# The first expert's rows: read back from slots, or gathered from the normalised tokens

## The chip, the core and the metric

The kernel runs on one core of a Trainium2 chip. The metric is device time in microseconds (us) of one execution, a median over runs. Five engines matter, each with an instruction queue of its own: PE (matrix products and transposes into PSUM banks), DVE (VectorE), ACT (ScalarE), POOL (GpSimd, which issues the indirect DMAs) and SP (SyncE, which issues the ordinary DMAs).

## What is computed

Two layers over 800 tokens (8 batches of 100) of width 512. Layer 0 is a cross attention and then a mixture of experts; layer 1 is a second cross attention and a quantised feed-forward. The change touches the mixture alone:

```python
scores = einsum('btd,ed->bte', layernorm(x), Wg)        # 8 experts
topk_s, topk_i = top_k(scores, 2); probs = softmax(topk_s)
for e in range(8):
    h = silu(xn @ W1[e].T) * (xn @ W2[e].T)             # 352 hidden
    y = y + w[..., e:e+1] * (h @ W3[e].T)
x = x + y
```

## The kernel before

The tokens stand in 7 tiles of 128 rows (the last has 32). The gate handles them in two groups, tiles 0 to 4 and tiles 5 and 6, so that the first group's work lies beside the last projections of attention 0.

For each group `gate_norm` (L583) writes the rows to `x_acc` in DRAM on SP (L585) and normalises them into `x_all` on DVE (L586). `gate_columns` and `gate_scores` make the scores on PE, `rank_choices` the two best experts of every token on DVE. `give_slots` (L677) then counts with two kinds of 0/1 products on PE (L682, L686) how many tokens chose each expert before this one, turns that into a slot number (`nb`, `slot`, `to`, L695 to L719 on DVE), and `scatter` (L699) has POOL write each tile's rows, once per choice, to their slots of the DRAM tensor `x_slot`: 10 indirect DMAs for the first group, 3 for the second (L700). Every expert owns 240 slots of 516 numbers: the 512 normalised values, two gate numbers, the rank and the token's number.

Between these steps stands the "fold", independent work for the second attention: for pairs of heads, `fold_first` (L732), `fold_turn` (L744), `fold_second` (L750) and `fold_third` (L761) alternate a few products on PE with a copy out of PSUM on ACT (L741, L748, L758, L765). The fold fills PE's time while the gate's small DVE chain runs. The order of PE, DVE and ACT is written out by hand in this region (`manual_schedule`); SP and POOL get theirs from the framework's planner, which places an instruction by its place in the program and the time it expects it to be ready.

After the second group's slots, one product counts all tokens per expert (L844); `most` and `spilt` (L846, L848) say if an expert got more than 240. All engines load `spilt` (L929) and branch on it (L936); the branch is not taken on these inputs. Behind the branch SP reads the slots of experts 0 and 1 back from `x_slot` (`fetch`, L1035, L1038), then loads the first weights to quantise (L874, L879). PE finishes the last fold (L1113 to L1116) and turns expert 0's rows to columns (`columns_of`, L1058, transposes at L1063, copies at L1065 and L1067). `choices` (L1043) makes the gate factor and the token number of each slot on DVE.

The loop over experts (L1119) does 48 products of 240 columns (L1126) and 12 of 512 (L1187) each, fetches expert e+2's slots, turns expert e+1's rows (L1165), quantises some weights of the last feed-forward on DVE, and adds the results into `x_acc` by indirect DMAs on POOL (L1199). Four row tiles (`slot_rows`, L920) hold the slots of two experts; the fetch for e+2 waits until the readers of expert e's tiles are done.

Of the kernel before, what the change touches and what calls it, by code (L numbers as in the profile page):

```python
# [50 lines left out]
def tile_kernel(  # L51
# [486 lines left out]
    def gate_col(tag, dtype=F32):  # L538
        return gp.tile([P, NT], dtype, tag=tag, name=tag)
# [39 lines left out]
    ms = [gate_col(f"m{k}") for k in range(2)]  # L579
    tops = [x_all[:, :, D + 2], gate_col("top1")]  # L580
    probs = [gate_col("p0"), x_all[:, :, D + 1]]

    def gate_norm(t):  # L583
        r = ROWS[t]
        nc.sync.dma_start(x_acc[ds(t * P, r), :], xs[t][:r])  # L585
        nc.vector.tensor_scalar(  # L586
            x_all[:r, t, :D], xs[t][:r], mvs[:r, t, 0:1], rstd_all[:r, t : t + 1],
            ALU.subtract, ALU.mult,
        )

    gate_in = []

    def gate_columns(t0, t1):
        if t0 == 0:
# [42 lines left out]
    def rank_choices(t0, t1):  # L639
# [34 lines left out]
        nc.vector.tensor_tensor(p2[:, g], p2[:, g], p1[:, g], ALU.mult)  # L674
        nc.vector.tensor_tensor(x_all[:, g, D], p1[:, g], p2[:, g], ALU.subtract)

    def give_slots(t0, t1):  # L677
# [18 lines left out]
        nc.vector.scalar_tensor_tensor(  # L696
            nb[:, g, :], counts, float(CAP), nb[:, g, :], ALU.is_lt, ALU.mult
        )
        def scatter(t, k, r):  # L699
            d = nc.gpsimd.indirect_dma_start(  # L700
                out=x_slot,
                out_offset=bass.IndirectOffsetOnAxis(ap=to_i[k][:r, t : t + 1], axis=0),
                in_=x_all[:r, t, :], in_offset=None,
            )
# [5 lines left out]
        n = t1 - t0  # L710
        nc.vector.tensor_tensor(
            tmp[:, :, g, :], hot[:, :, g, :],
            nb[:, g, :].unsqueeze(1).to_broadcast([P, 2, n, NE]), ALU.mult,
        )
        nc.vector.tensor_reduce(slot[:, :, g], tmp[:, :, g, :], AX.X, ALU.add)
        nc.vector.scalar_tensor_tensor(
            unfit[:, :, g], slot[:, :, g], 0.0, spill[:, :, g], ALU.is_equal, ALU.mult
        )
        nc.vector.tensor_tensor(to[:, :, g], unfit[:, :, g], slot[:, :, g], ALU.add)  # L719
        for k in range(2):  # L720
            for t in range(t0, min(t1, NT - 1)):
                scatter(t, k, ROWS[t])

        if t1 == NT:
            r = ROWS[-1]
            nc.vector.tensor_copy(x_all[ds(r, r), NT - 1, :], x_all[:r, NT - 1, :])
            nc.vector.tensor_copy(to_i[0][ds(r, r), NT - 1 :], to_i[1][:r, NT - 1 :])
            scatter(NT - 1, 0, 2 * r)

    def fold_first(t_p, *pairs):  # L732
        pa = bank()
        for n, (i, wq_p, kq_p, qr_p) in enumerate(pairs):
            for c in range(CQ // P):
                for j in range(2):
                    nc.tensor.matmul(
                        pa[ds(R1 * j, R1), ts(n, P)], qr_p[:, j, c, :], kq_p[:, j, c, :],
                        start=(c == 0), stop=(c == CQ // P - 1),
                    )  # L740
        nc.scalar.copy(t_p, pa[:, : 2 * P])  # L741
        return [(i, wq_p) for i, wq_p, _, _ in pairs], t_p
# [8 lines left out]
    def fold_second(i, wq_p, a_p):  # L751
        pb = bank()
        for j in range(2):
            nc.tensor.matmul(
                pb[ds(R1 * j, R1), :], a_p[:, ts(j, R1)], wq_p[:, j, :], start=True, stop=True
            )
# [66 lines left out]
    nc.scalar.activation(sd0[:, 0:1], ln_eps, AF.Exp)  # L823
    for t in range(5, 7):
        gate_norm(t)
    u3 = fold_first(turned[2], loaded.pop(0), loaded.pop(0))
    u2 = fold_turn(*u2)
    f0 = fold_second(*u1[0])
    xT = gate_columns(5, 7)
    u3 = fold_turn(*u3)  # L830
    f1 = fold_second(*u1[1])
    for i in (6, 7):
        loaded.append(fold_load(i))
    gate_scores(5, 7, xT, lambda: fold_third(*f0))
# [7 lines left out]
    pn = bank()  # L842
    for n, some in enumerate((first_group, both[:, 5, :], both[:, 6, :])):
        nc.tensor.matmul(pn[:, :NE], ones_bf, some, start=(n == 0), stop=(n == 2))  # L844
    most = small.tile([P, 1], F32, tag="most", name="most")
    nc.vector.tensor_reduce(most, pn[:, :NE], AX.X, ALU.max)  # L846
    spilt = gp.tile([P, 1], I32, tag="spilt", name="spilt")
    nc.vector.tensor_scalar(spilt, most, float(CAP), None, ALU.is_gt)  # L848
    f2 = fold_second(*u3[0])
    fold_third(*f1)  # L850
    turned = fw.tile([P, 2 * P], F32, tag="a_p", name="turned3", bufs=1)
    u4 = fold_first(turned, loaded.pop(0), loaded.pop(0))
# [56 lines left out]
    HC = len(SLOTS)  # L909
    GB = 3  # L910

    def quantise_next():
# [121 lines left out]

    def fetch(e, tiles=None):  # L1035
        got = []
        for i, xg in enumerate(tiles or slot_tiles(e)):
            d = nc.sync.dma_start(xg, x_slot[ds(1 + e * CAP + SLOTS[i][0], SLOTS[i][1]), :])  # L1038
            got.append((xg, d.ins))
        return got  # L1040

# [16 lines left out]
    def columns_of(e, got):  # L1058
        xgT = ffw.tile([P, KC, CAP], F32, tag="xgT", name=f"xgT{e}")
        for i, (s0, n) in enumerate(SLOTS):  # L1060
            pt = bank().rearrange("p (c q) -> p c q", c=KC)
            for c in range(KC):
                nc.tensor.transpose(pt[:, c, :n], got[i][0][:, ts(c, P)], ident[:n, :n])  # L1063
            if i % 2:
                nc.vector.tensor_copy(xgT[:, :, ds(s0, n)], pt[:, :, :n])  # L1065
            else:
                nc.scalar.copy(xgT[:, :, ds(s0, n)], pt[:, :, :n])  # L1067
        return xgT
# [7 lines left out]
    def load_wo(*heads):  # L1076
        for i in heads:
# [785 lines left out]
```

## Time and profile before

| what | us |
|---|---|
| median of 3 runs (lowest, highest) | 655.17 (654.39, 655.68) |
| the profiled execution's own time | 656.77 |
| its span, first to last instruction | 653.6 |
| PE busy in the span | 626.9 (96%) |
| DVE, ACT, POOL busy | 415.6, 242.4, 177.3 |
| span from 112 to 147.3 (the gate's end, up to expert 0's first product) | 35.3 |
| PE busy in 122 to 130 | 2.26 of 8.00 |
| PE busy in 135 to 141 | 4.28 of 6.00 |

Times are us from the span's first instruction. In a line of the timeline the first column is the start, the second how long the piece took, then come engine, line of the kernel, operation, what is written and read, and the number of instructions; in brackets stands the idle time of the engine before it and what ended it. PE's ends are modelled from the size of the product; the start of the engine that waited for the product is measured.

### The profile page before, as it was taken

How to read it: one execution, taken by the hardware profiler on the slowest of the kernel's cores; microseconds unless marked ns; L12 is line 12 of the kernel's file. 1: busy time of each engine (PE TensorE's matmuls, PEld its weight loads, DVE VectorE, ACT ScalarE, POOL GpSimd, SP SyncE). 2: the span in 40 equal slices, each digit the busy share in tenths (PEclk: the TensorE clock that was granted, in tenths of full speed). 3: DMA queues.
4: the chain of work that ended last, by engine and by line, in shares of the span. 5: the costliest groups of instructions: out<-in, count | busy, mean ns of one | idle time of the engine just before them, and what ended most of it. 6: DMA issues, size and time to landing. Idle time of an engine off the chain costs nothing.

```text
span 653.6 us, 9865 instructions
## 1 busy us (share of the span) xinstructions
PE 626.9 (96%) x3468; PEld 404.3 (62%) x3475; DVE 415.6 (64%) x1046; ACT 242.4 (37%) x554; POOL 177.3 (27%) x190
## 2 busy tenths in 40 slices
PE   9999999589999999999999999999999999999995
PEld 6767756347777776578866766666666544444442
DVE  4865688227777553245068877877676457666787
ACT  3653455351111111332255655555555213222130
POOL 1232430610222211128623234233243002222020
PEclk9999999799999999999999999999999999999998
DMA  8990184937999999553300212010000301011211
GB/s 294 306 253 18 57 265 142 308 118 237 295 297 328 286 258 299 120 184 113 89 1 17 61 44 61 17 37 12 1 12 0 127 11 26 20 20 30 51 38 65
DMA packets 80290, 80.34 MB, mean 123 GB/s; under 512 B 41267, under 2 KB 54119, under 8 KB 80111
## 3 DMA queue, kind: packets, MB, share of 16 engines
q1 hardware_dynamic: 76543, 70.97, 36.9%
q0 software_dynamic: 3696, 8.72, 5.9%
q8 instruction: 28, 0.46, 0.3%
q14 instruction: 23, 0.19, 0.1%
HBM read 56.36 MB, written 16.50 MB: 111 GB/s over the span
## 4 chain that ended last, share of the span: by engine, by line
PE 66%; DVE 6%; POOL 1%; DMA 1%; ACT 1%; issue 1%; ACTq 0%; SPq 0%; POOLq 0%; DVEq 0%
PE bank L384 12%; PE bank L1432 10%; PE bank L1126 9%; PE bank L1407 8%; PE bank L1349 7%; PE bank L1187 5%; PE bank L1424 5%; PE bank L1593 3%; PE bank L1227 2%; PE bank L1388 2%; DMA dn<-in_wdn 1%; POOL e L1418 1%; PE bank L1063 1%; DVE nm L1411 1%; DVE amax L152 1%
## 5 line engine op out<-in xcount | busy, mean ns | idle before, releaser
L1418 POOL TENSOR_SCALAR e<-e,rs 128x361 f32<-128x361 f32 x51 | 61.2, 1201 | 121.2 <-DVE rs L1417 85.0
L384 PE MATMUL bank<-wvo,ctxT 128*128 128x512 f32 x192 | 84.2, 593 | 0.0
L1407 PE MATMUL bank<-kvT,qe 128*128 128x361 f32 (+1 forms) x208 | 78.9, 475 | 0.9 <-ACT qe L1394 0.9
L1126 PE MATMUL bank<-xgT,w 128*128 128x240 f32 (+1 forms) x384 | 74.1, 369 | 0.4 <-ACT xgT L1067 0.4
L1126 PEld LDWEIGHTS bank<-xgT,w 128*128 128x128 f32 (+1 forms) x384 | 64.7, 181 | 11.5 <-issue 6.2
L1432 PE MATMUL bank<-pT,kvr 121*128 121x400 f32 x192 | 70.6, 503 | 0.0
L1415 ACT ACTIVATE e<-bank,nm 128x361 f32<-128x361 f32 x100 | 56.4, 564 | 33.4 <-DVE nm L1411 24.1
L1411 DVE TENSOR_REDUCE nm<-bank 128x1 f32<-128x361 f32 x100 | 52.7, 528 | 17.4 <-PE bank L1407 16.6
L1424 PEld LDWEIGHTS bank<-ident,e 128*121 128x121 f32 x300 | 46.6, 184 | 26.9 <-POOL e L1418 3.9
L384 PEld LDWEIGHTS bank<-wvo,ctxT 128*128 128x128 f32 x192 | 36.0, 190 | 42.1 <-issue 41.7
L1199 POOL DMA_INDIRECT x_acc<-y,place x16 | 24.7, 1542 | 108.1 <-ACT y L1198 105.4
L1610 POOL TENSOR_TENSOR hid<-g,u 128x512 f32<-128x512 f32 (+1 forms) x17 | 20.5, 1214 | 112.6 <-ACT g L1601 74.8
L1424 PE MATMUL bank<-ident,e 128*121 128x128 f32 x300 | 49.6, 275 | 1.0 <-POOL e L1418 1.0
L1432 PEld LDWEIGHTS bank<-pT,kvr 121*128 121x128 f32 x192 | 33.9, 190 | 20.6 <-ACT pT L82 0.9
L349 POOL TENSOR_TENSOR s<-s,rs 100x800 f32<-100x800 f32 x16 | 24.4, 1522 | 69.6 <-DVE rs L348 35.3
L1187 PE MATMUL bank<-w,hT 128*128 128x512 f32 (+3 forms) x96 | 42.9, 594 | 0.3 <-DVE hT L1150 0.3
L1407 PEld LDWEIGHTS bank<-kvT,qe 128*128 128x128 f32 (+1 forms) x208 | 32.1, 186 | 11.3 <-ACT qe L1394 2.2
L82 ACT COPY pT<-bank 121x384 f32<-121x384 f32 (+3 forms) x55 | 24.3, 442 | 25.0 <-PE bank L1424 24.4
L80 DVE COPY ctxT<-bank 128x400 f32<-128x400 f32 (+2 forms) x23 | 13.2, 572 | 30.5 <-PE bank L1349 24.9
L80 DVE COPY pT<-bank 121x384 f32<-121x384 f32 (+3 forms) x57 | 28.7, 503 | 2.3 <-PE bank L1424 2.3
L1349 PE MATMUL bank<-xT,wqf 128*128 128x256 f32 (+1 forms) x128 | 29.8, 393 | 0.0
L1593 PE MATMUL bank<-w1q,xqT 128*128 128x512 bf16 (+1 forms) x140 | 29.2, 361 | 0.4 <-DMA xqT<-xq 0.2
(267 smaller groups left out, 1002.8 us busy)
## 6 DMA issues: line engine op xcount, KB each, us to landing
w<-in_w SPq DMA_DIRECT2D x8, 1408.0 KB
gu<-in_wgu SPq DMA_DIRECT2D x22, 256.0 KB
wq_p<-in_wq SPq DMA_DIRECT2D x8, 512.0 KB
w<-in_w SPq DMA_DIRECT2D x16, 256.0 KB
wo<-in_wo SPq DMA_DIRECT2D x8, 512.0 KB
x_slot<-zeros SPq DMA_DIRECT2D x1, 3840.0 KB
kq_p<-in_wkcq SPq DMA_DIRECT2D x16, 192.0 KB
dn<-in_wdn SPq DMA_DIRECT2D x4, 704.0 KB
```

Of the source, the lines that this page charges most:

```text
L80: nc.vector.tensor_copy(dst, src)
L384: nc.tensor.matmul(po[:, :D], lhs[:, c, ds(t * P, r)], rhs[:, c, :], start=(c == 0), stop=(c == chunks - 1),)
L1126: nc.tensor.matmul(po, w12_e[:, c, cols], xgT[:, c, :], start=(c == c0), stop=(c == c1 - 1))
L1187: nc.tensor.matmul(py[i][:n], hT[:mr, m, ds(s0, n)], w3_e[:mr, m, :], start=(m == blocks[0]), stop=(m == blocks[2]),)
L1349: nc.tensor.matmul(pq[:, i, :], wqf[:, c, ts(p0 + i, P)], xT[:, c, :], start=(c == 0), stop=(c == KC - 1),)
L1407: nc.tensor.matmul(ps[ds(to, n), :L], qe[:, ds(k0, n)], kvT, start=True, stop=True)
L1411: d = nc.vector.tensor_reduce(nm[:r], ps[:r, :L], AX.X, ALU.max, negate=True)
L1415: nc.scalar.activation(e[:r], ps[:r, :L], AF.Exp, bias=nm[:r], accum_out=sm[:r])
L1418: (nc.vector if odd else nc.gpsimd).tensor_scalar_mul(e[:r], e[:r], rs[:r])
L1424: nc.tensor.transpose(pt[:LP, c, :r], e[:r, ds(c * (LP - 1), LP)], ident[:r, :r])
L1432: nc.tensor.matmul(pc[:, :VC], kvr[:, c, :], pT[:, c, :], start=(c == 0), stop=(c == LC - 1))
L1593: nc.tensor.matmul(pw[:r, :n], xqT[:, c, :r], w1q[:, c, ds(off, n)], start=(c == 0), stop=(c == KC - 1),)
```

## The change

1. Three constants on POOL: `count_up` (1 to 256 in every row) and `number` (per token its row, and its tile's first row).
2. `gate_norm` also writes the normalised rows to the DRAM tensor `x_all_rows`: 7 more DMAs on SP.
3. `give_slots` keeps `place_0`, the token's slot in expert 0 (0 if it has none). `is_slot` compares it with `count_up` on DVE: a 0/1 mask of 128 tokens by 256 slots for every tile, 5 ahead of the second group's columns and 2 within the second `give_slots`.
4. `add_tokens` multiplies each mask's transpose with `number` on PE and sums over the tiles in two PSUM banks (`found`): every slot gets its token's row and tile. There are 10 such products for the first group and 4 for the second; the fold step `f2` is moved ahead of the latter. Two reductions on DVE make whole numbers of them (`token_of`).
5. POOL gathers expert 0's 240 rows from `x_all_rows` by these numbers with two indirect DMAs, and only then issues the second group's 3 scatters (`to_slots`, now after the product L844, with its two small copies).
6. `most` and `spilt` come after that. The first weights' loads no longer wait for the fetches. Expert 0's fetch brings the last 4 columns only; `columns_of(0)` reads the gathered rows; `choices(0)` moves from ahead of the expert loop to the middle of expert 0, just ahead of `choices(1)`.

```diff
+    count_up = at.tile([P, 2 * P], BF16, tag="count_up", name="count_up")
+    nc.gpsimd.iota(count_up, pattern=[[1, 2 * P]], base=1, channel_multiplier=0, ...)
+    number = at.tile([P, NT, 2], BF16, tag="number", name="number")
...
     def gate_norm(t):
...
+        nc.sync.dma_start(x_all_rows[ds(t * P, r), :], x_all[:r, t, :D])
...
+    def is_slot(t0, t1):
+        for t in range(t0, t1):
+            nc.vector.tensor_scalar(
+                slot_of[:, t, :], count_up, place_0[:, t : t + 1], None, ALU.is_equal
+            )
+
+    def add_tokens(t0, t1):
+        for i in range(HC):
+            for t in range(t0, t1):
+                nc.tensor.matmul(
+                    found[i], slot_of[:, t, ts(i, P)], number[:, t, :],
+                    start=(t == 0), stop=(t == NT - 1),
+                )
...
     def give_slots(t0, t1):
...
+        nc.vector.tensor_tensor(place_0[:, g], nb[:, g, 0], both[:, g, 0], ALU.mult)
+        if t0:
+            is_slot(t0, t1)
...
     give_slots(0, 5)
+    to_slots(0, 5)
...
     for t in range(5, 7):
         gate_norm(t)
+    slot_of = at.tile([P, NT, 2 * P], BF16, tag="oT", name="slot_of")
+    is_slot(0, 5)
...
     f1 = fold_second(*u1[1])
+    found = [bank()[:, :2] for _ in range(HC)]
+    add_tokens(0, 5)
...
+    f2 = fold_second(*u3[0])
+    add_tokens(5, 7)
+    token_of = gp.tile([P, HC], I32, tag="token_of", name="token_of")
+        for i in range(HC):
+            nc.vector.tensor_reduce(token_of[:, i : i + 1], found[i], AX.X, ALU.add)
+    early = []
+    for i, (_, n) in enumerate(SLOTS):
+        xg = rows.tile([P, D], F32, tag="xn", name=f"early{i}")[:n]
+        gather = nc.gpsimd.indirect_dma_start(
+            out=xg, out_offset=None, in_=x_all_rows[:N, :],
+            in_offset=bass.IndirectOffsetOnAxis(ap=token_of[:n, i : i + 1], axis=0),
+        )
+        early.append((xg,))
+    behind_early = tc.issue_after(gather.ins)
+    behind_early.__enter__()
+    to_slots(5, 7)
+    behind_early.__exit__(None, None, None)
...
-    f2 = fold_second(*u3[0])
...
     def fetch(e, tiles=None):
         got = []
+        cols = slice(0 if e else D, W)
...
+    gate_up_in = [load_gate_up(gate_up_left.pop(0)) for _ in range(GB)]
+    down_in = load_down(0)
     slots = {e: fetch(e, first_tiles[e]) for e in range(2)}
...
-    gate_up_in = [load_gate_up(gate_up_left.pop(0)) for _ in range(GB)]
-    down_in = load_down(0)
...
-    turned = columns_of(0, slots[0])
+    turned = columns_of(0, early)
     fold_third(*folded[1])
-    gates = choices(0, slots[0])
...
-        slots.pop(e)
+        own = slots.pop(e)
...
+        if e == 0:
+            gates = choices(0, own)
         if e + 1 < NE:
             gates_next = choices(e + 1, slots[e + 1])
```

More of the change, by code (lines that the diff above doesn't have):

```diff
@@ L581, in tile_kernel @@
     probs = [gate_col("p0"), x_all[:, :, D + 1]]
+    count_up = at.tile([P, 2 * P], BF16, tag="count_up", name="count_up")
+    nc.gpsimd.iota(
+        count_up, pattern=[[1, 2 * P]], base=1, channel_multiplier=0,
+        allow_small_or_imprecise_dtypes=True,
+    )
+    number = at.tile([P, NT, 2], BF16, tag="number", name="number")
+    nc.gpsimd.iota(
+        number[:, :, 0], pattern=[[0, NT]], base=0, channel_multiplier=1,
+        allow_small_or_imprecise_dtypes=True,
+    )
+    nc.gpsimd.iota(
+        number[:, :, 1], pattern=[[P, NT]], base=0, channel_multiplier=0,
+        allow_small_or_imprecise_dtypes=True,
+    )
+    place_0 = gate_col("place_0")
     def gate_norm(t):
@@ L589, in gate_norm @@
         )
+        nc.sync.dma_start(x_all_rows[ds(t * P, r), :], x_all[:r, t, :D])
     gate_in = []
+    HC = len(SLOTS)
     def gate_columns(t0, t1):
@@ L675, in rank_choices @@
         nc.vector.tensor_tensor(x_all[:, g, D], p1[:, g], p2[:, g], ALU.subtract)
+    def is_slot(t0, t1):
+        for t in range(t0, t1):
+            nc.vector.tensor_scalar(
+                slot_of[:, t, :], count_up, place_0[:, t : t + 1], None, ALU.is_equal
+            )
+    def add_tokens(t0, t1):
[4 more added lines that the diff above has]
+                    start=(t == 0), stop=(t == NT - 1),
+                )
     def give_slots(t0, t1):
@@ L698, in give_slots, with to_slots @@
         )
+        nc.vector.tensor_tensor(place_0[:, g], nb[:, g, 0], both[:, g, 0], ALU.mult)
+        if t0:
+            is_slot(t0, t1)
+        n = t1 - t0
+        nc.vector.tensor_tensor(
+            tmp[:, :, g, :], hot[:, :, g, :],
+            nb[:, g, :].unsqueeze(1).to_broadcast([P, 2, n, NE]), ALU.mult,
+        )
+        nc.vector.tensor_reduce(slot[:, :, g], tmp[:, :, g, :], AX.X, ALU.add)
+        nc.vector.scalar_tensor_tensor(
+            unfit[:, :, g], slot[:, :, g], 0.0, spill[:, :, g], ALU.is_equal, ALU.mult
+        )
+        nc.vector.tensor_tensor(to[:, :, g], unfit[:, :, g], slot[:, :, g], ALU.add)
+    def to_slots(t0, t1):
+        if t1 == NT:
+            r = ROWS[-1]
+            nc.vector.tensor_copy(x_all[ds(r, r), NT - 1, :], x_all[:r, NT - 1, :])
+            nc.vector.tensor_copy(to_i[0][ds(r, r), NT - 1 :], to_i[1][:r, NT - 1 :])
         def scatter(t, k, r):
@@ L708, in scatter @@
             tc.add_to_no_dep_group("to_slots", d.ins)
[L710 to L719, printed above, removed]
         for k in range(2):
@@ L724, in give_slots @@
         if t1 == NT:
[L725 to L728, printed above, removed]
+            scatter(NT - 1, 0, 2 * ROWS[-1])
     def fold_first(t_p, *pairs):
@@ L844, in tile_kernel @@
         nc.tensor.matmul(pn[:, :NE], ones_bf, some, start=(n == 0), stop=(n == 2))
+    f2 = fold_second(*u3[0])
+    add_tokens(5, 7)
+    token_of = gp.tile([P, HC], I32, tag="token_of", name="token_of")
+    with nc.allow_low_precision(reason="sums of a row and its tile are whole numbers under 1024"):
+        for i in range(HC):
[6 more added lines that the diff above has]
+            in_offset=bass.IndirectOffsetOnAxis(ap=token_of[:n, i : i + 1], axis=0),
+        )
+        early.append((xg,))
[3 more added lines that the diff above has]
+    behind_early.__exit__(None, None, None)
     most = small.tile([P, 1], F32, tag="most", name="most")
@@ L908, in tile_kernel @@
     gate_up_left = list(range(OT - LATER))
-    HC = len(SLOTS)
     GB = 3
@@ L1036, in fetch @@
         got = []
+        cols = slice(0 if e else D, W)
         for i, xg in enumerate(tiles or slot_tiles(e)):
-            d = nc.sync.dma_start(xg, x_slot[ds(1 + e * CAP + SLOTS[i][0], SLOTS[i][1]), :])
+            d = nc.sync.dma_start(
+                xg[:, cols], x_slot[ds(1 + e * CAP + SLOTS[i][0], SLOTS[i][1]), cols]
+            )
             got.append((xg, d.ins))
```

## The prediction

> **What bounds the kernel now.** I read the page first: PE is busy for 626.9 of 653.6 us, so only PE's idle time can be won. The slices show where that lies.
>
> ```profile
> PE   9999999589999999999999999999999999999995
> DVE  4865688227777553245068877877676457666787
> POOL 1232430610222211128623234233243002222020
> ```
>
> A slice is 16.3 us. Slices 7 and 8 (114 to 147) are PE's only gap ahead of the last slice, and POOL's scatters stand in slice 7. From the next slice on, the experts keep PE full, so what PE loses before its first expert product (147.32) is lost for good.
>
> Next, the timeline of 112 to 150, PE and those that it waits for:
>
> ```profile
> 122.73 0.66 PE L764 MATMUL bank<-ident,f_p 128*128 128x128 f32 x4
> 128.42 0.33 DVE L624 COPY parts<-bank 128x160 f32<-128x160 f32 x1 [7.18 <-remote]
> 128.80 0.80 PE L629 MATMUL bank<-add_up,parts 128*128 128x8 f32 x4 [5.42 <-issue]
> 135.97 0.42 DVE L726 COPY x_all<-x_all 32x516 f32<-32x516 f32 x1
> 136.22 1.00 POOL L700 DMA_INDIRECT x_slot<-x_all,to  x1 [8.82 <-DVE to L719]
> 136.28 1.53 PE L737 MATMUL bank<-kq_p,qr_p 128*64 128x128 f32 x24
> 138.79 0.91 POOL L700 DMA_INDIRECT x_slot<-x_all,to  x1 [0.30 <-issue]
> 140.55 0.37 ACT L741 COPY turned<-bank 128x256 f32<-128x256 f32 x1 [3.58 <-PE bank L764]
> 140.98 0.44 PE L747 MATMUL bank<-ident,turned 128*128 128x128 f32 x2 [1.72 <-ACT turned L741]
> 141.54 1.76 SPq L1038 DMA_DIRECT2D xg<-x_slot  x4
> 143.15 1.94 PE L754 MATMUL bank<-wq_p,turned 128*64 128x512 f32 x8 [1.03 <-PEq L936]
> 145.02 0.66 PE L764 MATMUL bank<-ident,f_p 128*128 128x128 f32 x4
> 145.51 0.98 PE L1063 MATMUL bank<-ident,xg 128*128 128x128 f32 x8
> 147.32 9.31 PE L1126 MATMUL bank<-xgT,w 128*128 128x240 f32 x48 [0.38 <-ACT xgT L1067]
> ```
>
> Two things are to be seen. First, the slot path, POOL's scatters from 136.22 to 139.70, SP's fetch at 141.54, transposes at 145.51, does **not** hold PE: the transposes (145.51) follow straight on the fold's L764 (145.02 + 0.66, pipelined). By the trace's landing records the fetch of expert 0 has landed at 145.04, half a us before PE wants it. The path that the change shortens is already hidden, if only just. Second, what does hold PE is its own results reaching their readers late. L737 ends at 136.28 + 1.53 = 137.81 by the model, but ACT, idle and waiting for it, copies at 140.55: 2.74 late. L619 ended at about 122.80 and DVE reads it at 128.42: 5.6 late. Both stretches are those in which POOL issues scatters to the slots (114.66 to 127.39 and 136.22 to 139.70), and both end about 1 us after the last of them. In the expert stage, where POOL adds rows to another tensor, no such delay shows. I do not know the cause; I take the coincidence as the rule for the estimate.
>
> **The change, part by part.** The profiled execution took 656.77, span 653.6 plus 3.17 around it, 1.60 over the median of 655.17. I work out differences on its own timeline and add them to the median.
>
> *First group.* The three constants are of the kind of L557 and L562 (0.18 and 0.15 us); POOL is idle between 80.56 and 85.30, so they cost nothing; without that gap, 0.7 us. Seven DMAs of 256 KB at most, 1.64 MB, are added on SP. Five fall in 101 to 112, where the DMA share is 0.43; each costs SP about 0.4 us of issue (row L585, 0.34 to 0.42), ahead of weight loads that are used from 115 on. Two, 320 KB, fall in 116 to 131, when the queues are full (share 0.99, 328 GB/s in 122 to 130): 320/328 = 1.0 us more traffic. It ends in 130 to 135, where the share is 0.09: nothing, bound +1.0. Five masks on DVE: nearest row L586, a tensor_scalar of 512 f32 numbers, 0.54 us; half the numbers, 0.27 us, between 0.17 (the smallest DVE rows) and 0.43 (L148, 512 numbers to bf16). 5 x 0.27 = 1.35 us, and DVE has 3.69 us idle ahead of L607: nothing. Ten small products on PE, nearest row L686 and L844 (six with their weight loads in 0.4 us), stand in PE's 1.88 us ahead of L619: nothing; if that cover went, 0.7 us.
>
> *Second group, masks.* Here DVE is the path. Between L696 (ends 135.10) and L711 come `place_0` (0.17, row L695) and two masks (0.54), with 0.04 between: masks ready at 135.95. PE, free at 135.76 after the moved `f2`, waits behind them with its queue and runs 4 products (0.3): the fold step that began at 135.69 begins at 136.33. **+0.65** (bounds +0.4 and +1.0). Behind PE's wait stand the whole fold and the branch; ACT waits for the fold's banks.
>
> *POOL's order.* `token_of` needs two reductions (0.17 each) and stands at about 136.9; the gathers' first is issued at 137.0. No gather is in the trace; the nearest rows are the scatters, 0.96 plus 0.30 between, and for the far end L1199 at 1.54. Two gathers take 2.5 us, so the scatters go from 139.6 to 143.2 in place of 136.22 to 139.70: 3.4 later. The rows of `x_all_rows` have landed: even behind the fold's last load (issued 124.85, landed 131.21) they are there before 137.
>
> *The late result.* L737 now ends at 138.5, before the first scatter. If gathers do not delay PE's results, the wait of 1.72 at L747 goes: **-1.7** (bounds 0 and -1.72). What is late next is ACT's chain: the copy of L748, then L765 (0.58), the table load (1.28), a 0.20 activation, then L758, which PE waits for at L764. With the scatters at 139.6 to 143.2, L747's result (ready at 140.4) falls in their stretch. I price this with the row of the same kind, L737's lateness: **+2.7**. Bounds: 0 (nothing, as in the expert stage) and 5.6 (L619). I take 2.7, for it is the row with the same three scatters.
>
> *Behind the branch.* Expert 0's rows cost PE nothing before and after. Expert 1's slots wait for the scatters 3.4 us longer and stand behind 1.47 MB of first weights, some 5 us at 280 GB/s: landed at about 153 where 148.5 was; PE wants them at 156.55: nothing, with 3 us of cover. `choices(0)` moves from 147.13 to about 163, so the fetch of expert 2 (147.66 before) goes at about 164.3, behind the transpose issued at 163.08. The load issued at 164.33 landed at 171.54, the one at 164.99 at 172.88; PE wants expert 2's rows at 171.83 and 172.3. **+0.5** (bounds 0, and +3.3 if three weight loads go first and it lands at 175.6 as the fetch of expert 3 did).
>
> Sum: 0.65 - 1.7 + 2.7 + 0.5 = **+2.15**, 657.3.
>
> The first five masks also run beside POOL's scatters. The two scatters beside DVE work took 1.23 and 1.08 us, those beside an idle DVE 0.96: 0.12 to 0.27 more. The masks meet two scatters: bound +0.5, taken as nothing.
>
> A rule against the change, which the sum does without: the Trainium skill, "SBUF — State Buffer", section "Who interferes with whom", states that a DVE operation in a two-port mode locks GpSimd out of a shared port for its whole length, so that it can't write DMA descriptors meanwhile. Were the masks such operations, the first scatters would end up to 5 x 0.27 = 1.35 us later (an estimate by that page), and if PE's late results follow them the sum would be +3.5 in place of +2.15.
>
> **Rivals.**
> A. *Not slower: the lateness does not follow the scatters* (it comes from that one fold step, or from traffic that the gathers change). For it: the expert stage has POOL's adding scatters and no lateness; the cause is unknown. Against: both late stretches end with the slot scatters. Then 0.65 - 1.7 + 0.5 = -0.55, 654.6. It decides once the new lateness costs under 0.55 us.
> A2. *Faster*: as A, and expert 2's fetch is in time and the 0.38 ahead of L1126 goes: 0.65 - 1.7 - 0.38 = -1.4, 653.8. PE's idle time in 130 to 147.3 is 17.3 less 14.2 busy (5.00 + 4.28 + 1.12 + 3.78 in its stretches) = 3.1 in all, so with the masks' 0.65, -2.5 is the end, 652.7.
> B. *Gathers delay PE's results as scatters do.* Then L737's result waits until about 1 us after POOL's last issue, 144.1 in place of 140.55: +3.5, and +0.5 for expert 2's fetch: +4.0, 659.2. For it: the same engine and the same kind of instruction. Against: a gather reads DRAM and writes SBUF, as SP's loads do, which delay nothing in the expert stage.
> C. *SP blocks.* If expert 2's fetch keeps its place in SP's queue, ahead of the transposes and loads behind it, all of these wait from 148 to 163.5, and the weights that landed at 163.3 come some 11 us later. Expert 4's slots landed at 192.36 and are wanted at 202.3: 10 of cover for 11 of delay. So +1 on the forecast at least, +3.2, and +5 if several experts miss: 658.4 to 660. Against: the planner already takes loads out of the program's order (L511 ahead of the second L157).
> D. *The change does not do what it says*: the gathers wait for the rows' writes and go no sooner than the scatters did. Then PE waits at its transposes, as long as in B; its chance is counted there.
>
> **How the numbers follow.** Forecast (+0.9 to +3.2, by the bounds of the masks and of expert 2's fetch) 0.35; A 0.20; A2 0.20; B with D 0.17; C 0.08. A difference under 0.2%, 1.3 us, is about what a measurement of this kernel can't tell from none; 0.05 of the forecast lies in it, and all of A. So faster 0.20, same 0.25, slower 0.55. The range reaches from halfway into A2 to halfway into C: 653.4 to 660.0.
>
> **What would show it.** ACT's copy L741 after the fold's last first step at about 139 (right) or 144 (B); scatters of the second group from 139.6; ACT's L748 and L758 waiting 2 us or more for PE beside them; L1126's first start at 149 (forecast), 146.3 (A) or 151 (B); expert 2's transposes with a DMA wait before them. Wrong would be a first product of expert 0 before 147, or a loss that lies in another stage.

## The result and the profile after

| | before | changed |
|---|---|---|
| median of 12 executions (lowest, highest), us | 654.08 (651.68, 655.83) | 658.37 (655.80, 662.60) |
| ratio, 95% interval | | 1.0072 [1.0049, 1.0094] |
| profiled execution, its span | 656.77, 653.6 | 657.57, 655.8 |
| expert 0's first product | 147.32 | 149.79 |

The change costs 4.3 us. The profile of before lies 2.7 above its median and that of the changed kernel 0.8 below, so the two profiles differ by only 0.8 in time and 2.2 in span. They say where time goes; how much goes is read from the medians and from further profiles below.

The slices of the page that answer to those of before:

```profile
PE   8999999589999999999999999999999999999995
...
DVE  4865688235877544244168887876676457566787
...
POOL 1231430630112221118714324233243002222020
```

PE's hole in slices 7 and 8 (the first is slice 0) is as before; POOL's share of slice 8 rises from one tenth to three, with the gathers and the scatters behind them. The timeline of 121 to 150 of the changed kernel (start, duration, engine, line, operation, in brackets the idle time before and its releaser; L641 is L624 of before, L773 L737, L777 L741, L783 L747, L790 L754, L800 L764, L1123 L1063, L1184 L1126, L750 the scatter, L895 the gather). The "parts" are the second group's gate scores before they are summed, copied out of PSUM by DVE; the "fold's last first step" is the last call of `fold_first`:

```profile
129.68 0.33 DVE L641 COPY parts<-bank 128x160 f32<-128x160 f32 x1 [8.59 <-remote]
...
131.84 3.68 PE L790 MATMUL bank<-wq_p,turned 128*64 128x512 f32 x8
...
138.37 1.53 PE L773 MATMUL bank<-kq_p,qr_p 128*64 128x128 f32 x24
...
138.72 1.12 POOL L895 DMA_INDIRECT early<-x_all_rows,token_of  x1 [10.66 <-DVE token_of L891]
...
141.42 1.02 POOL L750 DMA_INDIRECT x_slot<-x_all,to  x1 [0.30 <-issue]
...
141.53 0.37 ACT L777 COPY turned<-bank 128x256 f32<-128x256 f32 x1 [2.46 <-PE bank L800]
...
141.95 0.44 PE L783 MATMUL bank<-ident,turned 128*128 128x128 f32 x2 [0.61 <-issue]
...
144.73 1.94 PE L790 MATMUL bank<-wq_p,turned 128*64 128x512 f32 x8 [1.12 <-PE bank L800]
...
147.80 0.98 PE L1123 MATMUL bank<-ident,early 128*128 128x128 f32 x8
...
149.79 0.44 PE L1184 MATMUL bank<-xgT,w 128*128 128x240 f32 x1 [0.56 <-ACT xgT L1127]
```

At 94 us, ahead of the change, the changed kernel is already 0.57 late (0.54 of it at 24 us). Less that, the shifts are: DVE's copy of the parts +0.69 (128.42 to 129.68), the fold's last first step L773 +1.52 (136.28 to 138.37), ACT's copy of it +0.41, expert 0's first product +1.90. So most of this loss is there **before** the first gather is issued. The wait in front of L641 is longer (8.59, before 7.18), and the steps behind it are slow: the same eight products L790 take 3.68 at 131.84 and 1.94 at 144.73. The windows show PE's clock beside it. Their columns are the window, its length, busy time and count of PE, PEld (its weight loads), DVE, ACT and POOL, then PE's granted clock (1.00 is full), the DMA share and GB/s. From 123 to 130, first before, then changed:

```profile
123.00:130.00 7.00, 1.58 (x10) 1.30 (x9) 0.65 (x4) 1.17 (x2) 3.48 (x4) 0.53 0.96 349
```

```profile
123.00:130.00 7.00, 0.00 (x0) 0.00 (x0) 0.32 (x1) 0.85 (x2) 3.85 (x4) 0.71 0.95 348
```

The trace shows no work of PE at all from 123 to 130, and by windows of 1 us it then works at a clock of 0.50 until about 136.2 (133.7 in the profile of before).

Among the experts PE waits once, 0.86 in expert 2's additions (in the profile of before once, 0.30 in expert 3's), and every later addition is +3.03 instead of +2.47:

```profile
194.79 1.98 PE L1247 MATMUL bank<-w,hT 96*128 96x512 f32 x4 [0.86 <-DVE hT L1208]
```

### The profile page after: what moved, and what is told of

It reads as the page before. It is cut to its first block, busy times and chain, and to the rows that moved or that the text cites. A ratio compares the mean times of both kernels' runs of the same rounds, so it can differ in the third digit from the quotient of the medians.

```text
span 655.8 us, 9932 instructions
## 1 busy us (share of the span) xinstructions
PE 627.4 (96%) x3489; PEld 405.0 (62%) x3489; DVE 417.3 (64%) x1057; ACT 243.0 (37%) x554; POOL 180.1 (27%) x195
## 4 chain that ended last, share of the span: by engine, by line
PE 80%; DVE 8%; ACT 3%; DMA 3%; POOL 2%; issue 2%; another core or an unknown queue 1%; SPq 0%; ACTq 0%; DVEq 0%; POOLq 0%
PE bank L384 14%; PE bank L1492 10%; PE bank L1184 9%; PE bank L1467 8%; PE bank L1409 7%; PE bank L1247 5%; PE bank L1484 5%; PE bank L296 3%; PE bank L1653 3%; PE bank L1287 2%; PE bank L1448 2%; DMA dn<-in_wdn 2%; PE bank L790 1%; DMA wq_sb<-in_wq 1%
## 5 line engine op out<-in xcount | busy, mean ns | idle before, releaser
L1184 PE MATMUL bank<-xgT,w 128*128 128x240 f32 (+1 forms) x384 | 74.1, 369 | 0.6 <-ACT xgT L1127 0.6
L1184 PEld LDWEIGHTS bank<-xgT,w 128*128 128x128 f32 (+1 forms) x384 | 64.7, 181 | 11.7 <-issue 6.2
L1247 PE MATMUL bank<-w,hT 128*128 128x512 f32 (+3 forms) x96 | 42.9, 594 | 0.9 <-DVE hT L1208 0.9
L1247 PEld LDWEIGHTS bank<-w,hT 128*128 128x128 f32 (+3 forms) x96 | 17.0, 183 | 20.9 <-issue 15.4
```

Source lines behind the costliest of these rows:

```text
L1184: nc.tensor.matmul(po, w12_e[:, c, cols], xgT[:, c, :], start=(c == c0), stop=(c == c1 - 1))
L1247: nc.tensor.matmul(py[i][:n], hT[:mr, m, ds(s0, n)], w3_e[:mr, m, :], start=(m == blocks[0]), stop=(m == blocks[2]),)
```

## The experiments

The theory to test was the prediction's: PE's results come late while POOL issues scatters to the slots, the masks cost PE 0.65, and the first group's additions hide. Rivals: the row writes (W), the masks and small products of the first group (M), the moved fetches and `choices(0)` among the experts. "Net" is a shift less the difference at the first scatter; for the first pair of profiles the 0.57 is taken off. Each profile is one execution.

### Four kernels on a chip where no result is late

The kernel before took 648.92 on this chip (35 executions), 5 us less than on the first. It was not profiled here, and the changed kernel was not run here as it is.

**e1_writes**, the kernel before plus the row writes:

```diff
+        nc.sync.dma_start(x_all_rows[ds(t * P, r), :], x_all[:r, t, :D])
```

> The kernel before plus only the seven writes of normalised rows to x_all_rows. Profile times are us from the span's start, shifts are against the profile of before (which holds 0.57 of start-up difference to the one after at 94 us; that is taken off). Theory W (the writes' traffic lengthens the stretch in which PE's results come late): DVE's copy of the second group's parts (128.42 before) comes 0.5 to 0.7 later, the half clock behind it lasts longer, expert 0's first product (147.32) comes 1.0 to 1.6 later, and the time is 0.15 to 0.25% above the kernel before. Rival M (the masks and small products do it): all of these within 0.3 us of before, the time within 0.1%.

649.15, ratio 1.0017 [1.0004, 1.0031]. The time lies in theory W's range, but neither reading fits: the copy of the parts (L625 here, L624 of before) is not late at all, and what PE loses is a wait that neither named.

```profile
120.90 0.33 DVE L625 COPY parts<-bank 128x160 f32<-128x160 f32 x1 [1.49 <-PE bank L620]
...
126.52 1.09 PE L738 MATMUL bank<-kq_p,qr_p 128*64 128x128 f32 x14
...
131.42 1.30 PE L738 MATMUL bank<-kq_p,qr_p 128*64 128x128 f32 x9 [3.81 <-DMA qr_p<-in_wqr]
...
132.97 0.37 ACT L742 COPY turned<-bank 128x256 f32<-128x256 f32 x1 [5.75 <-PE bank L738]
```

PE stops after 14 of 24 products for the last weight `qr_p`. With two more writes in SP's queue the planner puts this small load behind two loads of 512 KB: issued at 121.29, landed by 131.28. Without the writes (e2) it is issued at 117.50 and landed by 123.38.

**e2_numbers**, the kernel before plus constants, masks, products and `token_of`, the fold step `f2` ahead of the last products:

```diff
+        nc.vector.tensor_tensor(place_0[:, g], nb[:, g, 0], both[:, g, 0], ALU.mult)
+        if t0:
+            is_slot(t0, t1)
...
+    is_slot(0, 5)
...
+    add_tokens(0, 5)
...
+    add_tokens(5, 7)
```

> The kernel before plus constants, masks, the 14 small products, the reductions to token_of and the moved fold step, with no writes, no gathers, and the scatters where they were. Theory W: DVE's copy of the parts stays at 128.4 to 128.7, only the second group's two masks and four products show, 0.3 to 0.65, and expert 0's first product comes 0.3 to 0.7 later; the time is 0.05 to 0.1% above before. Rival M: the copy comes 0.5 to 0.7 later and the first product 1.5 to 2.0 later, the time 0.25% above before.

646.74, ratio 0.9966 [0.9943, 0.9988]: faster. The copy stands at 120.77, nothing waits for `qr_p`, the second group's masks hold PE for 0.37, and expert 0's first product comes at 138.18. That work was added and time fell is not explained. Its time goes with PE's mean granted clock over the execution: eleven of its twelve were granted 0.995 to 0.999 and the kernel before 0.989 to 0.998, and at 0.998 they took 645.57 to 646.35 and 646.00.

**e3_scatters_first**, the changed kernel with the scatters ahead of the gathers:

```diff
     give_slots(5, 7)
+    last = to_slots(5, 7)
...
-    behind_early = tc.issue_after(gather.ins)
-    behind_early.__enter__()
-    to_slots(5, 7)
+    behind_early = tc.issue_after(last.ins)
+    behind_early.__enter__()
+    early = []
```

> The changed kernel with the second group's three scatters issued ahead of the two gathers. If it is POOL's scatters alone that make PE's results late, the scatters stand at about 138.5 to 142, ACT's copy behind the fold's last first step comes 2.7 late instead of 1.6, what follows is no longer late, and the gathers (issued 142 to 144.5, landed 148) make the first expert's transposes wait up to 0.5: first product between 149.3 and 150.3, the time within 0.1% of the changed kernel. If gathers delay PE's results as scatters do, the whole chain up to the table load stands later as well and the first product comes at 150.5 to 151.5, 0.15 to 0.25% above the changed kernel. If neither delays PE and only the wait for rows counts: 149.8 + 0.3.

650.32, 1.0031 [1.0009, 1.0054]. Scatters at 128.09 to 131.58, gathers to 134.15, and PE waits 4.11 for `qr_p`; ACT's copy (133.93) is late for that reason alone. The question of late results can't be answered on a chip that has none, and this version was not run on another.

**e4_choices_back**, the changed kernel with part 6 taken back except for the gathered rows:

```diff
-    gate_up_in = [load_gate_up(gate_up_left.pop(0)) for _ in range(GB)]
-    down_in = load_down(0)
     slots = {e: fetch(e, first_tiles[e]) for e in range(2)}
     behind_slots = tc.issue_after(slots[1][-1][1])
     behind_slots.__enter__()
+    gate_up_in = [load_gate_up(gate_up_left.pop(0)) for _ in range(GB)]
+    down_in = load_down(0)
...
+    gates = choices(0, slots[0])
     for e in range(NE):
```

> The changed kernel with the loads of the first weights behind the slots' fetches again, and choices(0) ahead of the expert loop again. Theory: nothing behind the branch costs anything, so expert 0's first product (149.8) and the time stay within 0.3 us and 0.1% of the changed kernel. Rival (the moved choices and the late fetch of expert 2 cost the 0.56 that PE's wait for DVE's hT grew by at 195): that wait is back at 0.3 us and the time is 0.5 to 0.9 us below the changed kernel.

649.24, 1.0013 [0.9994, 1.0033]. The rival's wait is gone, as it has it: PE has no wait among the experts, and from expert 0's first product to expert 7's first addition on POOL it takes 121.26. It is 122.00 in e3, and on the first chip 122.39 in the changed kernel and 121.83 in the kernel before. The rival's gain in time could not be tested, for want of the changed kernel on this chip.

### The two kernels as they are, on a chip with late results

**e5_before_again** (no edit) and **e6_after_again** (no edit):

> The kernel before, unchanged, for a profile beside the experiments on the chip they ran on; its ratio to itself shows the noise (1.000 within 0.2%). If PE's late results behind the first group's scatters belong to the kernel, DVE's copy of the second group's parts stands at 128 again (5 us or more of waiting); if they belong to the chip or to the recording of the first profile, it stands at 121, as in the four experiments, and expert 0's first product comes at 139 to 142.

> The changed kernel, unchanged. In the four experiments the fold's last first step waited for a weight (qr_p), which SP issues behind two 512 KB loads once the two row writes of the second group stand in its queue: 2.4 to 4.1 us of PE waiting with the writes, none without. Theory Q (the planner puts the weight behind the loads): PE waits 2.4 to 4 us there, expert 0's first product comes 1 to 3 us later than in the kernel before on the same chip, and the ratio is 1.002 to 1.006. Rival (late results behind POOL's scatters): no wait for a load there, but ACT and DVE waiting for PE's results, in both kernels.

656.53, 0.9992 [0.9973, 1.0010], and 661.23, 1.0074 [1.0046, 1.0102], against 656.24. The late results are back, the copy of the parts first of all (e5, then e6, which has a late copy behind the moved scatters too):

```profile
128.92 0.32 DVE L624 COPY parts<-bank 128x160 f32<-128x160 f32 x1 [7.20 <-remote]
```

```profile
129.22 0.32 DVE L641 COPY parts<-bank 128x160 f32<-128x160 f32 x1 [8.77 <-remote]
...
144.94 0.59 ACT L801 COPY wqf<-bank 128x512 f32<-128x512 f32 x1 [2.04 <-remote]
```

No wait for `qr_p`, for PE comes to it at 137.32 when it has long landed. Net of the first scatter (115.10 and 114.59): parts +0.81, the fold's last first step +1.66, expert 0's first product +2.43 (148.87 to 150.79). From there to expert 7's first addition 121.26 and 123.04, **+1.78**. By windows of 1 us PE's clock is 0.50 a second time behind the branch, until 146.6 in e5 and 148.1 in e6, which it was not in the first pair. In e6 among the experts (L1247 and L1208 are L1187 and L1150 of before):

```profile
190.74 1.62 DVE L152 TENSOR_REDUCE amax<-dn 128x1 f32<-128x1408 f32 x1 [1.93 <-DMA dn<-in_wdn]
...
196.45 1.98 PE L1247 MATMUL bank<-w,hT 96*128 96x512 f32 x4 [1.52 <-DVE hT L1208]
```

DVE waits for a weight to quantise, and its part of the hidden product is queued behind. The moved `choices(0)` holds expert 0's tiles, so expert 2's fetch goes at 166.93 instead of 149.21, into the stretch in which the queues are full; the load `dn`, issued at 180.42 (178.04 in e5), lands at 190.72 (184.16).

**e7_rows_later**, the changed kernel with the second group's row writes behind the fold's loads:

```diff
     for i in (6, 7):
         loaded.append(fold_load(i))
+    for t in range(5, 7):
+        write_rows(t)
```

> The changed kernel with the writes of rows 640 to 799 placed after the fold's last loads, so that SP issues the weight qr_p ahead of the two 512 KB loads, as in the kernel before. Theory Q: qr_p lands at about 123 instead of 131, PE's wait for it is gone, the gathers wait for the rows instead (issued at 131 to 132 in place of 128.3), the first expert product comes 1 to 3 us earlier than in the changed kernel, and the time is 0.2 to 0.5% lower. Rival W (it is the writes' traffic, or POOL's instructions): no earlier first product, the same time within 0.1%.

661.28, 1.0082 [1.0053, 1.0110]: as e6. `qr_p` now goes at 117.74, and it makes no difference, since PE comes at 138.34. The rest of theory Q fails too: the gathers go at 138.69, and expert 0's first product comes at 152.00, net 3.30 behind e5 (e6 2.43); up to the fold's last first step it is 2.34. From the first product to expert 7's addition it takes 123.37. On the chip where the wait for `qr_p` held PE this version was not run.

### Which part costs, and whether the scatters do it

Another chip, where the kernel before takes 653.62 (23 executions).

**e8_numbers_again**, the edit of e2:

> The kernel before plus constants, masks, small products, token_of and the moved fold step, without the row writes and gathers: once more, since the chip of its first run showed no late results and this one may. Where results are late: if the two row writes lengthen the first late stretch (DVE's copy of the parts 1.6 to 1.9 after POOL's last scatter of the first group with the whole change, 1.0 to 1.1 without), it is 1.0 to 1.1 here, and expert 0's first product comes 0.3 to 0.7 later than in the kernel before; if the masks and products lengthen it, 1.6 to 1.9 and 1.0 to 1.6 later. Where none is late: as before, the time 0.2 to 0.4% under the kernel before.

657.25, **1.0048 [1.0031, 1.0065]**: the numbers (the constants, the masks, the small products, the reductions and the moved fold step) cost 3 us here, without a write or a gather. Its profiled execution (651.34) is not like its other ten (656.34 to 657.90): there DVE's copy of the parts came at 123.42, only 2.4 after its product's end (120.99), and 4.2 before the group's last scatter ended (127.58), so a late result need not last as long as the scatters. So the size is shown, its place in the other ten is not.

**e9_no_first_scatters**, the kernel before with the first group's scatters left out, and **e11_before_third** (no edit):

```diff
-        for k in range(2):
+        for k in range(2 if t0 else 0):
             for t in range(t0, min(t1, NT - 1)):
```

> The kernel before without the first group's ten scatters (their tokens' rows never reach the slots, so this part of the mixture is left out). If POOL's scatters make PE's results late, DVE's copy of the second group's parts comes at 121 to 122 where it came at 128.4 to 128.9, PE's clock stays at 1.00, the second group's scatters still make the copy behind the fold's last first step 2.7 late, and expert 0's first product comes 5 to 7 us earlier. If the lateness belongs to the load traffic of that stretch, the copy still waits to 125 or later. On a chip that shows no lateness the copy stands at 121 with and without them.

> The kernel before, unchanged, for the profile on this chip. Where results are late: DVE's copy of the parts at 128.4 to 128.9, first product of expert 0 at 147 to 149. Where none is late: the copy at 121 and the first product at 139 to 142, and something there makes the kernel before 2 us slower than with the numbers added, which its waits name.

One execution each, 649.05 (below all 23 of the kernel before) and 654.99. First e9, then e11, the timelines and the window of 123 to 130:

```profile
120.90 0.33 DVE L624 COPY parts<-bank 128x160 f32<-128x160 f32 x1 [1.49 <-PE bank L619]
...
126.53 1.53 PE L737 MATMUL bank<-kq_p,qr_p 128*64 128x128 f32 x24
...
127.50 1.23 POOL L700 DMA_INDIRECT x_slot<-x_all,to  x1 [28.88 <-DVE spilt L848]
...
128.11 0.37 ACT L741 COPY turned<-bank 128x256 f32<-128x256 f32 x1 [0.88 <-PE bank L737]
...
137.87 0.63 PE L1063 MATMUL bank<-ident,xg 128*128 128x128 f32 x4 [3.97 <-DMA xg<-x_slot]
...
140.20 7.01 PE L1126 MATMUL bank<-xgT,w 128*128 128x240 f32 x28
```

```profile
127.64 0.32 DVE L624 COPY parts<-bank 128x160 f32<-128x160 f32 x1 [6.44 <-remote]
...
135.72 1.53 PE L737 MATMUL bank<-kq_p,qr_p 128*64 128x128 f32 x24
...
139.19 0.37 ACT L741 COPY turned<-bank 128x256 f32<-128x256 f32 x1 [2.78 <-PE bank L764]
...
146.48 0.85 PE L1126 MATMUL bank<-xgT,w 128*128 128x240 f32 x3 [0.38 <-ACT xgT L1067]
```

```profile
123.00:130.00 7.00, 7.00 (x61) 3.88 (x58) 3.86 (x24) 4.25 (x10) 2.19 (x2) 1.00 0.19 70
```

```profile
123.00:130.00 7.00, 2.29 (x13) 1.67 (x13) 1.06 (x6) 1.27 (x3) 3.53 (x4) 0.76 0.97 352
```

Take the ten scatters away and the late stretch is gone, with it the half clock of that stretch, and the first product comes 6.3 earlier although PE now waits 3.97 for its slots (its clock is 0.50 behind that wait, until 142.4). (The DMA share falls too; that the scatters' data rather than POOL's issuing is to blame is not excluded.) But the second half of the rule falls: the second group's three scatters stand here at 127.50 to 131.24, and L741's copy comes 0.05 after its product ends (126.53 + 1.53), where e11 has 1.94. Here three scatters by themselves make nothing late.

**e10_both_back**, the edits of e4 and e7 together:

> The changed kernel with the row writes of the second group behind the fold's last loads (the weight qr_p goes first), and with the first weights' loads and choices(0) back where the kernel before has them. The moved choices and fetches cost the changed kernel 0.56 to 1.8 us among the experts (a load for the third quantised weight comes late and DVE's part of the hidden product with it). Theory: that part is gone, from expert 0's first product to expert 7's addition it takes 121.3, as in the kernel before; the rest stays, so 1.002 to 1.005 of the kernel before where results are late. Rival: it is the chip's noise, and the ratio stays at 1.007. Where no result is late and nothing waits for qr_p: 0.997 to 1.000.

656.52, 1.0043 [1.0026, 1.0060], as the theory has it. Against e11, whose first scatter starts within 0.01 of it (L646, L778 and L1192 are L624, L737 and L1126 of before):

```profile
129.13 0.32 DVE L646 COPY parts<-bank 128x160 f32<-128x160 f32 x1 [8.64 <-remote]
...
137.45 1.53 PE L778 MATMUL bank<-kq_p,qr_p 128*64 128x128 f32 x24
...
148.96 1.25 PE L1192 MATMUL bank<-xgT,w 128*128 128x240 f32 x5 [0.66 <-ACT xgT L1134]
```

Parts +1.49, fold step +1.73, first product +2.48; 121.97 from there to expert 7's addition, not the 121.3 expected, with a wait of 0.45 for DVE in expert 0.

### A version that the experiments point to

The gathers make expert 0 independent of the slots, so the first group's scatters can leave the stretch in which they hurt. **e12_scatters_last** is e7 with seven of the ten behind the gathers:

```diff
     give_slots(0, 5)
-    to_slots(0, 5)
+    to_slots(0, 5, [(0, t) for t in range(3)])
...
+    to_slots(0, 5, [(k, t) for k in range(2) for t in range(5) if k or t >= 3])
     to_slots(5, 7)
...
-    close_gp()
...
+    close_gp()
     close_ffw()
```

> The changed kernel with the row writes of the second group behind the fold's last loads, and with seven of the first group's ten scatters moved behind the two gathers, ahead of the second group's three: only three scatters stand beside the gate's second group. The gate's tensors stay allocated to the end of the experts, so that nothing waits for the scatters' reads. Theory (POOL's row of scatters makes PE's results late, and the gathers free the scatters to go elsewhere): DVE's copy of the second group's parts at 121 to 122 where the kernel before has 127.6 to 128.9 on chips with late results; gathers at 127.5 to 130; scatters 130 to 143; expert 0's first product at 136 to 140 instead of 146.5 to 148.9. Expert 1's slots land at about 147.5 and are wanted 9.3 after the first product, so PE waits 0 to 3 us there; in sum 4 to 8 us earlier than the kernel before, ratio 0.988 to 0.995. Rival (the late results only move with the scatters, to the fold's last steps and the first expert): the copy at 121, but expert 0's first product at 143 or later, ratio 0.998 to 1.005. On a chip without late results: ratio 0.998 to 1.004, for PE then waits for expert 1's slots.

661.06, 1.0110 [1.0087, 1.0134] on a fourth chip (654.05 before): slower, and no better than the changed kernel's 1.0072 and 1.0074 on other chips. The rival's place (143 or later) came, but not for its reason and not its ratio. Half of the theory holds, the half that decides does not:

```profile
120.81 0.33 DVE L646 COPY parts<-bank 128x160 f32<-128x160 f32 x1 [1.42 <-PE bank L641]
...
134.50 0.98 PE L1131 MATMUL bank<-ident,early 128*128 128x128 f32 x8
...
147.98 0.59 ACT L1135 COPY xgT<-bank 128x512 f32<-128x512 f32 x1 [11.90 <-DMA xg<-x_slot]
...
148.89 12.26 PE L1192 MATMUL bank<-xgT,w 128*128 128x240 f32 x48 [12.97 <-DVE xgT L1133]
```

The copy of the parts is in time and expert 0's gathered rows are turned at 134.50, 11 us earlier than the transposes in the profile of before. Then ACT's copy of the columns stands still until 147.98. Its semaphores include that of the last scatter, which lands at 146.66; ACT and DVE get past this semaphore at 147.31, 0.66 later. The columns' tile belongs to a pool (a region of SBUF that tiles are allocated from) opened behind the branch, and its first writer waits for everything that came before, gate or not. The wait costs twice: PE's clock is 0.50 behind it until 154.9, and expert 0's 48 products take 12.26 instead of 9.31. Keeping the gate's tensors allocated did not lift it. In the changed kernel the same wait is there, and it is not hidden: the last scatter has landed at 147.55, ACT gets past its semaphore at 148.21, again 0.66 later, and copies at 148.88, 1.08 after the transposes began; in e10 it is 146.72, 147.38 and 1.18. Where the scatters had landed in good time (before, e5, e11, e6, e7) the copy comes 0.82 to 0.88 after them. So the wait costs the changed kernel 0.20 and e10 0.30. (Whether results are late on this chip was not seen: the kernel before was not profiled on it.) A version with that wait removed was not tried, so no version of the gathers here is shown to beat the kernel before.

## Why the prediction held, and where its steps did not

The sign is right and 657.3 is near the 658.37 measured, but the loss was put at 2.15 and is 4.3: the first three executions of the kernel before (655.17) lay above its later median. So the near figure is partly luck: half the loss on a base 1.1 too high. By the loss alone, rivals B (+4.0) and C (+3.2 and more) were nearer. The first group was taken as nothing and cost, the masks of the second and the pair behind them were taken too large.

- **The slot path does not hold PE, and the change frees nothing there.** Right. PE goes from L800 straight to the transposes in both kernels, and expert 1's slots landed at 155.23 and were wanted at 159.03.
- **Results come late because of POOL's scatters.** Right for the ten of the first group (e9 beside e11, one execution each), on chips where it happens at all. Too broad for the three of the second group (e9). And the estimate let the gathers delay nothing: in the changed kernel, e6, e7 and e10, with the gathers alone beside it, ACT's copy comes 1.63 to 1.68 after its product and 0.42 to 0.48 after the second gather ends.
- **The first group's additions are hidden (0).** This is the step that failed. Up to L773 the changed kernel loses 1.52, 1.66 and 1.73 net in three pairs of profiles (before and changed, e5 and e6, e11 and e10; 2.34 with e7 beside e5), of which the second group's masks are 0.28: 1.2 to 1.5 come from the first group in the three pairs. The copy of the parts comes 1.6 to 1.9 after POOL's last scatter of the group instead of 0.2 to 1.1 (e7 included), and the half clock ends later with it. By time the numbers alone, without writes, cost 3 us (e8); that number holds the second group's masks too. I had covered the masks and products by idle time of DVE and PE, but ahead of the late copy those engines were idle because they were waiting, and that wait grew (7.18 to 8.59 on DVE). How masks or products lengthen it stays open. (The DMA share of 0.43 that I gave for 101 to 112 is that of 95 to 112; for 101 to 112 it is 0.58.)
- **Second group's masks, +0.65.** Measured +0.28: `nb` moves by 1.84, the fold step behind masks and products by 2.12. The two masks took 0.48 and the products 0.40, but the moved `f2` fills PE for most of it.
- **The gathers.** 1.12 and 0.96 with 0.31 between; 2.5 was reckoned for 2.7. They start at 138.72 instead of 137.0, for the reason above.
- **L747's wait -1.7, new lateness behind the scatters +2.7.** Measured: the wait falls from 1.72 to 0.61, and L777 still comes 1.63 after its product (2.74 before). From L773 to the first product the net loss is 0.38, 0.77 and 0.75, where the two terms gave +1.0; 0.20 and 0.30 of the first and the last are the wait for the last scatter, which I did not have. The lateness behind the moved scatters shows in e6 and e7, where ACT waits 2.04 and copies 1.08 and 1.05 after the last of them; in the changed kernel and e10 it waits 0.61 and 0.34. The direction holds, both sizes are too large. The forecast had ACT's copy L741 at 139 and rival B at 144; it stands at 141.53, delayed beside the gathers as B has it, but not to the end of the scatters. Rival A would have had a gain; there is none.
- **Behind the branch, +0.5 for expert 2's fetch.** The size of the first pair is 0.56, of the second 1.78. From expert 0's first product to expert 7's addition it takes 122.00 to 123.37 in the four profiles with part 6 (changed, e3, e6, e7), and without it 121.26 or 121.27 in six, 121.83 in the first of before, 121.97 in e10 (e9 and e12 aside, where PE's clock is 0.50 in expert 0). Taking it back moves the ratio from 1.0074 to 1.0043, but on two chips and with intervals that overlap. The object was wrong: expert 2's rows came in time (landed by 170.28, wanted at 174.24), and a weight for DVE was late in their place. Rival C did not come: the planner put that fetch behind the transposes and loads, so SP was not blocked, but the transfers behind it were later.
- **The rule against the change** (the Trainium skill, "SBUF — State Buffer", "Who interferes with whom") shows once at most: the five masks took 1.05 and meet the second and third scatter, which took 1.06 and 0.96 (1.08 and 0.96 before). In e8 alone the second took 1.39.
- Not seen at all: the planner's reordering of `qr_p` (2.4 to 4.1 us of PE where nothing else is late), the copy's wait for the last scatter (0.20 to 0.30), and that PE's clock falls in its waits (the same eight products 3.68 and 1.94).

By times on the chips with late results: numbers alone +0.48%, everything but part 6 +0.43%, everything +0.72 and +0.74%. So the numbers cost about 3 us, which e8 shows; that part 6 costs about 2, and writes, gathers and the new order together about nothing, is read from differences of these ratios, and the chips differ.

## What to carry to other kernels

Idle time in which an engine waits for something that is itself slow is no cover: ask what ends the wait, and whether the added work moves that end. Before data are fetched by another way to get rid of a wait, list every semaphore of the first writer behind it, for a tile of a newly opened pool can wait for the very transfers that were bypassed. A load or store that costs a queue nothing can still change the order in which a planner issues the others.

## What the runs showed of the hardware

- How late PE's results come differs between chips, and on one of them between executions (e8). On one, the parts were copied at 120.77 to 121.53 in all four kernels, with ten scatters beside them, and the kernel before takes 648.92; where results were late it takes 653.62 to 656.24. In the late profiles the trace also lost records: the transfers issued between 113 and 123 have 0 to 10 of their 16 landing records, against 12 to 16 on the chip without lateness. In e9 the second group's first two scatters kept 5 and 7 of 16 records and nothing was late, so lost records alone do not make a result late. Whether taking the records has a part in the lateness is open, for no execution here is without them.
- After waits of 4.0 to 13 us PE ran at a clock of 0.50 (3.97 in e9, 5.42 in before, 7.56 in the changed kernel, 12.97 in e12), and it took 3.6 to 6.2 us until it was 1.00 again (before 128.80 to 133.7, changed 130.06 to 136.2; in e12, with PE busy throughout, 148.89 to 154.9). Eight products of 512 columns took 2.84 to 3.68 instead of 1.94.
- A gather of 128 or 112 rows of 2 KB held POOL for 0.96 to 1.12 us. With all 16 landing records it had landed 3.4 to 3.5 us after its start in e3 and 4.1 and 5.1 in e4; elsewhere the last record that was kept came 2.9 to 3.7 after it.
- A copy with eighteen semaphores spent 0.67 us on ACT checking them, about 0.08 for each step of two.
